# Depthwise convolution as three products over half columns, four channels in four row groups of TensorE

## The chip, the cores and the metric

The kernel runs on one core of a Trainium2 chip. The metric is device time in microseconds (us) of one execution. The median of 13 runs of the kernel before is 4737.9 us (4729.0 to 4768.0). A core has five engines: TensorE (PE, with its weight loads as PEld), VectorE (DVE), ScalarE (ACT), GpSimd (POOL) and SyncE (SP), which in this program only issues DMA transfers. ScalarE and GpSimd issue some transfers too.

## The reference

Two layers in a row, all in float32. The first layer takes x of shape (32 images, 128 channels, 56, 56):

```python
x = conv(input, dw_kernel)          # 7x7, one filter per channel, padding 3
x = layernorm over the 128 channels of each pixel
logits = x @ Wg; top 2 of 8 experts per token, softmax weights, at most CAP tokens an expert
out = input + x + layer_scale * (sum over the token's experts of gate * MLP(x))
```

The second layer is a coordinate attention (two pooled directions, two sigmoid gates), a full 3x3 convolution, a batch norm and a SiLU on the same shape. The change is in the first line alone: y[n, c, h, w] = bias[c] + sum over i, j of k[c, i, j] * x[n, c, h + i - 3, w + j - 3].

## The kernel before

The program runs in stages, and in one instruction order per engine that follows the order of the code where the tile framework's scheduler has no reason to differ. The stages are: the depthwise convolution (lines 99 to 156, writes y_d in HBM), the layer norm with the routing scores (lines 163 to 312, reads y_d back), the experts (gathers, two matrix products and accumulating scatters, lines 613 to 646), and the second layer (from line 802). Only the first is touched.

**The depthwise convolution before.** It takes two channels at a time, 64 pairs. The 56 rows of an image lie on 56 partitions: one channel on partitions 0 to 55, the other on 64 to 119 (`rows`). The free axis of the tile `xt` holds 32 images x 56 columns. A column tap of the filter is a product of `xt`, shifted along the columns, with a banded 56 x 56 matrix (`band`, a diagonal per row tap), so seven taps sum up the 7x7 filter in PSUM. Images are split in two halves, which go to the lower and the upper 64 partitions of the output, so that four matmuls (two channels, two halves) use the four 64 x 64 quarters of the array. An accumulator `acc` holds 2 x 8 images x 56 columns of one channel in one PSUM bank; there are 8 banks, and a pair of channels uses 4 of them, two in each of two turns (`b`).

Around the products:

- SP loads `hk` (the taps, line 123) and `xt` (line 124), one transfer each per channel. `xt` has three buffers, so a load waits until TensorE is done with the pair three before.
- GpSimd reverses `hk` into `band` (line 125).
- ScalarE evicts the accumulator of the first channel with its bias (line 148), VectorE that of the second (line 150), into `yt` (three buffers).
- ScalarE issues the writes of `yt` to y_d: four per pair, of 196 KB each, after the second turn's evictions (line 153). Every run of 56 columns is a packet of 224 B, in the loads of x as in the writes of y_d.

The next stage loads y_d with SP (line 263) and can do so only when the last write has landed.

Transfers that SP and ScalarE issue signal through eight semaphores that they take in turn; a transfer that takes a semaphore again first waits until that semaphore's previous transfer has landed.

Of the kernel before, what the change touches and what calls it, by code (L numbers as in the profile page):

```python
# [8 lines left out]
F32 = mybir.dt.float32  # L9
# [3 lines left out]
AF = mybir.ActivationFunctionType  # L13
ALU = mybir.AluOpType
# [4 lines left out]
N, C, H, W = 32, 128, 56, 56  # L19
# [5 lines left out]
P = 128  # L25
# [14 lines left out]
WIN = 2 * H - 1  # L40


def bc(ap, shape):
    return ap.to_broadcast(shape)
# [3 lines left out]
def moe_conv_then_coordatt_kernel(ctx: ExitStack, tc: tile.TileContext, a: dict, out: bass.AP):  # L48
    nc = tc.nc
# [6 lines left out]
    y_d = dram.tile([N, C, HW], F32, name="y_d")  # L56
# [41 lines left out]

    with ExitStack() as st:
        cp1 = st.enter_context(tc.tile_pool(name="dwc", bufs=1))  # L100
        xp = st.enter_context(tc.tile_pool(name="dwx", bufs=3))
        wp = st.enter_context(tc.tile_pool(name="dww", bufs=3))
        yp = st.enter_context(tc.tile_pool(name="dwy", bufs=3))
        pp = st.enter_context(tc.tile_pool(name="dwp", bufs=8, space=PSUM))

        G = P // 2
        dwb = cp1.tile([P, C], F32, name="dwb")
        nc.sync.dma_start(dwb, a["dw_bias"].rearrange("c h -> (c h)").unsqueeze(0).partition_broadcast(P)
                          .rearrange("p x c -> p (x c)"))
        taps = a["dw_kernel"]  # L110
        NB = 4
        NI = N // NB
        bands = [cp1.tile([P, 7, G], F32, name=f"band_{k}") for k in range(3)]
        for t in bands:
            nc.gpsimd.memset(t, 0.0)
        for cp in range(C // 2):
            hk = wp.tile([P, 7, H], F32, tag="hk", name=f"hk{cp}")
            xt = xp.tile([P, N, W], F32, tag="xt", name=f"xt{cp}")
            band = bands[cp % 3]
            for c in range(2):  # L120
                rows = slice(c * G, c * G + H)
                src = bass.AP(taps.tensor, taps.offset + (2 * cp + c) * 7 * WIN, [[1, H], [WIN, 7], [1, H]])
                nc.sync.dma_start(hk[rows], src)
                nc.sync.dma_start(xt[rows], a["x"][:, 2 * cp + c].rearrange("n h w -> h n w"))
                nc.gpsimd.tensor_copy(band[rows, :, 0:H], hk[rows, :, ::-1])  # L125
            yt = yp.tile([P, 2, N // 2, W], F32, tag="yt", name=f"yt{cp}")
            for b in range(NB // 2):

                acc = [pp.tile([P, NI, W], F32, tag="acc", name=f"acc{cp}_{b}_{c}") for c in range(2)]
                for n, dw in enumerate((3, 0, 1, 2, 4, 5, 6)):  # L130
                    s = dw - 3
                    lo, hi = max(0, -s), W - max(0, s)
                    for half in range(2):
                        im = slice(half * N // 2 + b * NI, half * N // 2 + (b + 1) * NI)
                        for c in range(2):
                            rows = slice(c * G, c * G + H)
                            nc.tensor.matmul(  # L137
                                acc[c][half * G : (half + 1) * G, :, lo:hi],
                                lhsT=band[rows, dw, :],
                                rhs=xt[rows, im, lo + s : hi + s],  # L140
                                start=(n == 0),
                                stop=(n == 6),
                            )
                for c in range(2):
                    ch = c * (C // 2) + cp
                    dst = yt[:, c, b * NI : (b + 1) * NI, :]
                    if c == 0:
                        nc.scalar.activation(dst, acc[c], AF.Identity, bias=dwb[:, ch : ch + 1])
                    else:
                        nc.vector.tensor_scalar(dst, acc[c], dwb[:, ch : ch + 1], None, ALU.add)  # L150
            for half in range(2):
                for c in range(2):
                    nc.scalar.dma_start(
                        y_d[half * N // 2 : (half + 1) * N // 2, 2 * cp + c, :].rearrange("n (h w) -> h n w", h=H),
                        yt[half * G : half * G + H, c],
                    )

    pr_stack = ExitStack()
    prp = pr_stack.enter_context(tc.tile_pool(name="prp", bufs=1))
# [3 lines left out]
    with ExitStack() as st:  # L163
        yp = st.enter_context(tc.tile_pool(name="lny", bufs=2))
        cp1 = st.enter_context(tc.tile_pool(name="lnc", bufs=4))
        qp = st.enter_context(tc.tile_pool(name="lnq", bufs=1))
        xp = st.enter_context(tc.tile_pool(name="lnx", bufs=2))
        sp = st.enter_context(tc.tile_pool(name="lns", bufs=3))
        pp = st.enter_context(tc.tile_pool(name="lnp", bufs=8, space=PSUM))
# [10 lines left out]
        yts = {}  # L180
# [136 lines left out]
    with ExitStack() as st:  # L317
# [242 lines left out]
        cp1 = st.enter_context(tc.tile_pool(name="fc", bufs=1))  # L560
        wp = st.enter_context(tc.tile_pool(name="fw", bufs=2))
        xp = st.enter_context(tc.tile_pool(name="fx", bufs=1))
# [63 lines left out]
        def back(e, i, yt, xg, idx):  # L626

            pb = pbp.tile([P, BLK, C], F32, tag="pb", name=f"pb{e}_{i}")
            for k, (t, n) in enumerate(blocks[i]):
                nc.tensor.transpose(pb[0:n, k, :], yt[:, k * P : k * P + n], ident)  # L630
            nb, t0 = len(blocks[i]), blocks[i][0][0]
            c = max(c for c in range(NC_) if CHUNKS[c] <= i)
            turn_, k_ = (e * NC_ + c) % 2, i - CHUNKS[c]
            yo = yo_all[turn_][k_]
            whole = [x for x in blocks[i] if x[1] == P]
            parts = [(0, len(whole), P)] if whole else []
            parts += [(k, k + 1, n) for k, (t, n) in enumerate(blocks[i]) if n < P]
            for k0, k1, n in parts:
                shape = [n, k1 - k0, C]
                nc.vector.tensor_tensor(yo[0:n, k0:k1, :], pb[0:n, k0:k1, :], bc(xg[0:n, k0:k1, C + e : C + e + 1], shape),  # L640
                                        ALU.mult)
            return yo
# [14 lines left out]
        def load_weights(e):  # L657
            w1 = wp.tile([C, FF], F32, tag="w1", name=f"w1_{e}")
            nc.sync.dma_start(w1, a["W1"][e])
            w2 = wp.tile([P, NF, C], F32, tag="w2", name=f"w2_{e}")  # L660
            nc.sync.dma_start(w2, a["W2"][e].rearrange("(f p) c -> p f c", p=P))
            return w1, w2

        def weights(e, w1, w2):

            nc.gpsimd.tensor_tensor(w2, w2, bc(ls_bc.unsqueeze(1), [P, NF, C]), ALU.mult)
            pb = php.tile([P, BLK * P], F32, tag="ph", name=f"pb_{e}")[:, 0:NF]
            for f in range(NF):
                nc.tensor.matmul(pb[:, f : f + 1], lhsT=w1[:, f * P : (f + 1) * P], rhs=beta_c, start=True, stop=True)
            bias = wp.tile([P, NF], F32, tag="bias", name=f"bias_{e}")  # L670
            nc.vector.tensor_tensor(bias, pb, b1[:, e, :], ALU.add)
            return w1, w2, bias
# [57 lines left out]
        def some_routing(n):  # L730
            nonlocal issued
            n = min(n, len(order) - issued)
            issued += n
            return order[issued - n : issued]
# [39 lines left out]
        w = weights(0, *load_weights(0))  # L774
        for e in range(E):
# [8 lines left out]
            steps = [some_routing(n) for n in PIECES[e > 0]]  # L784
            compute(e, 0, w, steps[0])
            if e + 1 < E:
                w = weights(e + 1, *load_weights(e + 1)), w
            else:
                w = None, w
# [3 lines left out]
            w = w[0]  # L793
# [8 lines left out]
    with ExitStack() as st:  # L802
        cp1 = st.enter_context(tc.tile_pool(name="cc", bufs=1))
        xp = st.enter_context(tc.tile_pool(name="cx", bufs=2))
# [4 lines left out]
        mp = st.enter_context(tc.tile_pool(name="cm", bufs=3))  # L809
# [72 lines left out]
        for k in range(2):  # L882
            t = cp1.tile([C, H + 2, W + 2], F32, name=f"pad{k}")
# [193 lines left out]
```

## Time and profile before

| | |
|---|---|
| median of 13 runs | 4737.9 us |
| profiled execution | 4743.9 us |
| its span | 4742.0 us |
| depthwise convolution: first to last matmul | 9.9 to 676.4 us |
| load of y_d for the next stage issued | 684.0 us |
| PE busy over the span | 3692.5 us (78%) |
| DVE, ACT, POOL busy | 2174.3, 1313.5, 2688.4 us |
| granted TensorE clock, mean over the span and in the convolution | 0.87 and 1.00 |
| DMA in the convolution from 100 to 600 us | 176 GB/s, nearly all packets under 512 B |

How to read it. A fence that begins with a number is a row of a stretch or of the order of time, in microseconds from the span's start. In the list of groups a row gives line, engine, operation, output and inputs by the program's names, partitions x elements, the count, then busy time, the mean of one in ns, and the idle time of the engine in front of these instructions with what ended it. A float32 matmul shows as two records, so 7168 records are 3584 matmuls. Matmuls overlap and their ends are modelled, so "busy" is not "at its peak". An ACTq or SPq row is the time that an engine takes to issue a transfer, not the time that the transfer takes. The DMA share is the mean over 16 DMA engines of the time that packets took, which can pass 1 where packets overlap.

### The profile page before, as it was taken

Reading aid. Unit: us, or ns where it says so; the run is one execution under the profiler, and the core shown is the slowest. Engines: PE = TensorE matmul, PEld = TensorE weight load, DVE = VectorE, ACT = ScalarE, POOL = GpSimd, SP = SyncE. Lnnn points to the kernel's source line nnn. Section 1 sums busy time; section 2 is a strip of 40 time slices with the busy share of each in tenths; the row PEclk is TensorE's granted clock in tenths of the full one; section 3 lists DMA queues with packets and bytes.
Section 4 is the critical chain, followed back from the end, with each engine's and each line's share of the span. In section 5 each row is a group of like instructions: output and inputs, shape, how many; then the busy total and the mean of one; then the engine's idle time right before and its main releaser. Section 6 shows DMA issues by size and latency. Waiting matters only on the chain. (4 is left out here: it accounts for less than half of the span.)

```text
span 4742.0 us, 50118 instructions
## 1 busy us (share of the span) xinstructions
PE 3692.5 (78%) x17669; PEld 2062.6 (43%) x17669; DVE 2174.3 (46%) x4727; ACT 1313.5 (28%) x2555; POOL 2688.4 (57%) x1862
## 2 busy tenths in 40 slices
PE   9999989774167748656765886677664899999999
PEld 4555558774133324333432343233332455555555
DVE  1111108988736526636441110011113878787776
ACT  1111117553012212212222332232221233333333
POOL 1011003344067868767767766787785765666655
PEclk9999999877578878777877898888887999999999
DMA  9999978987222223222323332233335343444432
GB/s 156 176 177 176 177 165 293 336 314 262 83 44 38 38 51 35 39 44 39 41 41 42 39 47 42 48 41 42 47 42 126 124 156 127 150 150 151 148 123 76
DMA packets 866353, 526.90 MB, mean 111 GB/s; under 512 B 543880, under 2 KB 835488, under 8 KB 855648
## 3 DMA queue, kind: packets, MB, share of 16 engines
q1 hardware_dynamic: 504848, 327.79, 24.1%
q0 software_dynamic: 118720, 91.19, 14.1%
q10 hardware_dynamic: 242320, 102.85, 9.6%
q8 instruction: 155, 2.54, 0.2%
q14 instruction: 310, 2.54, 0.2%
HBM read 268.72 MB, written 252.97 MB: 110 GB/s over the span
## 5 line engine op out<-in xcount | busy, mean ns | idle before, releaser
L646 POOL DMA_INDIRECT acc_d<-yo,idx x676 | 1080.8, 1599 | 311.8 <-issue 205.8
L613 PE MATMUL ph<-fxt,w 128*128 128x512 f32 (+1 forms) x1400 | 714.1, 650 | 259.6 <-ACT ht L614 228.3
L614 ACT ACTIVATE ht<-ph,bias 128x512 f32<-128x512 f32 (+1 forms) x700 | 476.9, 683 | 858.9 <-PE ph L613 439.2
L982 PE MATMUL pc<-v,wk 128*128 128x392 f32 x1920 | 696.3, 505 | 3.2 <-POOL v L967 3.2
L137 PE MATMUL acc<-xt,band 56*64 56x424 f32 (+3 forms) x7168 | 666.4, 527 | 2.7 <-DMA xt<-in_x 2.7
L621 PE MATMUL py<-ht,w 128*128 128x512 f32 (+1 forms) x1400 | 649.3, 608 | 0.0
L594 POOL DMA_INDIRECT xg_r<-x_d,idx x556 | 536.9, 966 | 181.4 <-issue 119.9
L613 PEld LDWEIGHTS ph<-fxt,w 128*128 128x128 f32 x1400 | 274.5, 210 | 547.4 <-issue 287.4
L137 PEld LDWEIGHTS acc<-xt,band 56*64 56x64 f32 x7168 | 339.1, 132 | 329.4 <-issue 215.0
L982 PEld LDWEIGHTS pc<-v,wk 128*128 128x128 f32 x1920 | 344.4, 189 | 307.1 <-issue 96.1
L962 POOL TENSOR_TENSOR d<-pad 128x3248 f32<-128x3248 f32 x32 | 228.3, 7136 | 408.5 <-DVE pad L954 408.5
L275 PE MATMUL lnps<-proj,lnyt 128*128 128x136 f32 x1568 | 361.0, 398 | 103.8 <-ACT sq L280 74.5
L640 DVE TENSOR_TENSOR yo<-pb,xg_r 128x512 f32<-128x512 f32 (+2 forms) x147 | 98.3, 671 | 666.6 <-PE pb L630 279.8
L275 PEld LDWEIGHTS lnps<-proj,lnyt 128*128 128x128 f32 x1568 | 349.4, 316 | 116.0 <-ACT sq L280 85.6
L125 POOL COPY band<-hk 56x392 f32<-56x392 f32 x128 | 65.2, 510 | 573.2 <-issue 520.3
L621 PEld LDWEIGHTS py<-ht,w 128*128 128x128 f32 x1400 | 266.2, 199 | 278.6 <-issue 276.7
L150 DVE TENSOR_SCALAR yt<-acc,dwb 128x448 f32<-128x448 f32 x128 | 87.5, 684 | 582.2 <-PE acc L137 353.5
L605 DVE COPY fxt<-pt 128x512 f32<-128x512 f32 (+1 forms) x175 | 119.5, 683 | 493.9 <-PE pt L603 247.5
L623 ACT ACTIVATE fyt<-py,b 128x512 f32<-128x512 f32 (+1 forms) x175 | 119.6, 683 | 813.6 <-PE py L621 472.9
L992 DVE SCALAR_TENSOR_TENSOR y<-pc,y 128x392 f32<-128x392 f32 x640 | 318.2, 555 | 32.4 <-PE pc L982 32.4
L412 PE MATMUL ps_r<-cnt_r,ones 128*128 128x1 f32 x400 | 83.3, 289 | 248.3 <-DVE junk L411 170.5
L630 PE MATMUL pb<-ident,fyt 128*128 128x128 f32 (+1 forms) x696 | 117.7, 295 | 168.5 <-ACT fyt L623 93.2
(221 smaller groups left out, 4512.1 us busy)
## 6 DMA issues: line engine op xcount, KB each, us to landing
x_d<-xn SPq DMA_DIRECT2D x16, 3332.0 KB
xt<-in_x SPq DMA_DIRECT2D x128, 392.0 KB
y_d<-yt ACTq DMA_DIRECT2D x256, 196.0 KB
lnyt<-y_d SPq DMA_DIRECT2D x16, 3136.0 KB
acc_d<-xn SPq DMA_DIRECT2D x16, 3136.0 KB
x<-in_x SPq DMA_DIRECT2D x16, 3136.0 KB
cxn<-acc_d SPq DMA_DIRECT2D x112, 448.0 KB
out<-y ACTq DMA_DIRECT2D x64, 784.0 KB
```

The source lines that it names most:

```text
L137: nc.tensor.matmul(acc[c][half * G : (half + 1) * G, :, lo:hi], lhsT=band[rows, dw, :], rhs=xt[rows, im, lo + s : hi + s], start=(n == 0), ...
L275: nc.tensor.matmul(ps[:, j, :], lhsT=yf[:, self.j0 + g + j, :], rhs=proj, start=True, stop=True)
L594: d = nc.gpsimd.indirect_dma_start(out=xg[0:n, k, :], out_offset=None, in_=x_d[:, :], in_offset=bass.IndirectOffsetOnAxis(ap=idx[0][0:n, t ...
L605: nc.vector.tensor_copy(xt[:, 0:N_], pt[:, 0:N_])
L613: nc.tensor.matmul(ph[:, 0:N_], lhsT=w[0][:, f * P : (f + 1) * P], rhs=xt[:, 0:N_], start=True, stop=True)
L614: nc.scalar.activation(ht[:, f, 0:N_], ph[:, 0:N_], AF.Gelu, bias=w[2][:, f : f + 1])
L621: nc.tensor.matmul(py[:, 0:N_], lhsT=w2[:, f, :], rhs=ht[:, f, 0:N_], start=(f == 0), stop=(f == NF - 1))
L623: nc.scalar.activation(yt[:, 0:N_], py[:, 0:N_], AF.Identity, bias=b2[:, e : e + 1])
L646: d = nc.gpsimd.indirect_dma_start(out=acc_d[:, :], out_offset=bass.IndirectOffsetOnAxis(ap=idxs[e][1][0:n, t : t + 1], axis=0), in_=yo[0: ...
L962: nc.gpsimd.tensor_tensor(d, high, low, ALU.subtract)
L982: nc.tensor.matmul(m[k], lhsT=wk[k][:, dw, :], rhs=v[:, k, rows, dw : dw + W], start=(dw == 0), stop=(dw == 2))
L992: nc.vector.scalar_tensor_tensor(r[x], m[k], f, r[y_], ALU.mult, ALU.add)
```

## The change

The image rows now lie two to a partition: partition g of a channel holds rows 2g and 2g + 1, 28 partitions a channel, and four channels lie on partitions 0 to 27, 32 to 59, 64 to 91 and 96 to 123. A load of x has packets of two rows, 448 B, still 392 KB a channel.

The columns are split into even and odd ones, E and O, 28 each. A row filter of seven taps over all columns is made of three products over half columns: one with the sums E + O and the middle taps, which both output halves need, one with the odd columns and differences of taps, for the even outputs, and one with the even columns, for the odd outputs. The products have 3, 4 and 4 column offsets, and each offset two row parities: 22 products of 16 images x 28 columns, for two image halves, per channel. (Before: 7 taps of 8 images x 56 columns, in two turns, for two halves.)

There are 32 groups of four channels. In a group, each step of a product issues eight matmuls: four channels on four groups of 32 rows of the array, two image halves on two groups of 64 columns. Each channel has an accumulator in a bank of its own, so a product takes four of the 8 banks.

- ScalarE evicts the first product of each channel with the bias into `m0` (4 evictions a group); VectorE evicts the other two, adds `m0` and writes every second column of `yt` (8 a group).
- GpSimd makes three pieces of `band` with a copy and two subtractions and adds up `xs` = E + O (1792 elements a partition) for each group, one group ahead. Before the first group it clears three tiles `xt`, three `hk` and two `band`.
- ScalarE issues the eight writes of a group (196 KB each, as before) after VectorE's evictions of the third product. In the built program ScalarE's order is: four evictions of a group, its eight writes, four evictions of the next group.
- `yt` and `m0` have eight buffers, `xt` and `hk` three, `band` and `xs` two.

Rows of the new code, with the lines of the old one that they replace left out:

```diff
+        PRODUCTS = ((0, (0, -1, 1), -1), (3, (0, -2, -1, 1), -2), (7, (0, -1, 1, 2), -1))
+                nc.sync.dma_start(hk[rows, 1:8, :], bass.AP(taps.tensor, taps.offset + c * 7 * WIN, [[2, GH], [WIN, 7], [1, K1]]))
+                nc.sync.dma_start(xt[rows].rearrange("g n a w -> g n (a w)"),
+                                  a["x"][:, c].rearrange("n (g a) w -> g n (a w)", a=2))
...
+            nc.gpsimd.tensor_copy(band[:, 0:3, 0:K1], back(2, 8))
+            nc.gpsimd.tensor_tensor(band[:, 3:7, 0:K1], back(1, 9), back(0, 8), ALU.subtract)
+            nc.gpsimd.tensor_tensor(band[:, 7:11, 0:K1], back(1, 9), back(2, 9), ALU.subtract)
+            nc.gpsimd.tensor_tensor(xs, xt[:, :, :, 0:W:2], xt[:, :, :, 1:W:2], ALU.add)
...
+            sources = (xs, xt[:, :, :, 1:W:2], xt[:, :, :, 0:W:2])
+            for i, (t0, offsets, least) in enumerate(PRODUCTS):
+                acc = [pp.tile([P, N // 2, WH], F32, tag="acc", name=f"acc{q}_{i}_{r}") for r in range(QC)]
+                steps = [(o, par) for o in offsets for par in range(2)]
+                for n, (o, par) in enumerate(steps):
+                    lo, hi = max(0, -o), WH - max(0, o)
+                    for r in range(QC):
+                        rows = slice(32 * r, 32 * r + GH)
+                        for half in range(2):
                             nc.tensor.matmul(
+                                acc[r][half * M : (half + 1) * M, :, lo:hi],
+                                lhsT=band[rows, t0 + o - least, 1 - par : 1 - par + M],
+                                rhs=sources[i][rows, half * N // 2 : (half + 1) * N // 2, par, lo + o : hi + o],
...
+                for r in range(QC):
+                    if i == 0:
+                        nc.scalar.activation(m0, acc[r], AF.Identity, bias=dwb[:, k : k + 1])
...
+                    else:
+                        nc.vector.tensor_tensor(yts[r][:, :, i - 1 : W : 2], acc[r], common[r], ALU.add)
+                    if i == 2:
+                        for half in range(2):
+                            nc.scalar.dma_start(
+                                y_d[half * N // 2 : (half + 1) * N // 2, c, :].rearrange("n (h w) -> h n w", h=H),
+                                yts[r][half * M : half * M + H],
+                            )
```

More of the change, by code (lines that the diff above doesn't have):

```diff
@@ L100, in moe_conv_then_coordatt_kernel @@
         cp1 = st.enter_context(tc.tile_pool(name="dwc", bufs=1))
-        xp = st.enter_context(tc.tile_pool(name="dwx", bufs=3))
-        wp = st.enter_context(tc.tile_pool(name="dww", bufs=3))
-        yp = st.enter_context(tc.tile_pool(name="dwy", bufs=3))
+        mp = st.enter_context(tc.tile_pool(name="dwm", bufs=8))
+        yp = st.enter_context(tc.tile_pool(name="dwy", bufs=8))
         pp = st.enter_context(tc.tile_pool(name="dwp", bufs=8, space=PSUM))
-        G = P // 2
+        GH, WH, QC = H // 2, W // 2, 4
+        K1 = H + 1
+        NQ_ = C // QC
+        M = P // 2
         dwb = cp1.tile([P, C], F32, name="dwb")
@@ L110, in moe_conv_then_coordatt_kernel @@
         taps = a["dw_kernel"]
[L111 to L114, printed above, removed]
-            nc.gpsimd.memset(t, 0.0)
[L116 to L136, printed above, removed]
@@ new lines, in moe_conv_then_coordatt_kernel, with fetched @@
+        xts = [cp1.tile([P, N, 2, W], F32, name=f"xt{k}") for k in range(3)]
+        xss = [cp1.tile([P, N, 2, WH], F32, name=f"xs{k}") for k in range(2)]
+        hks = [cp1.tile([P, 9, K1], F32, name=f"hk{k}") for k in range(3)]
+        bands = [cp1.tile([P, 11, M + 1], F32, name=f"band{k}") for k in range(2)]
+        for t in xts + hks + bands:
+            nc.gpsimd.memset(t, 0.0)
+        PRODUCTS = ((0, (0, -1, 1), -1), (3, (0, -2, -1, 1), -2), (7, (0, -1, 1, 2), -1))
+        def fetched(q):
+            xt, hk = xts[q % 3], hks[q % 3]
+            for r in range(QC):
+                c = QC * q + r
+                rows = slice(32 * r, 32 * r + GH)
+                nc.sync.dma_start(hk[rows, 1:8, :], bass.AP(taps.tensor, taps.offset + c * 7 * WIN, [[2, GH], [WIN, 7], [1, K1]]))
+                nc.sync.dma_start(xt[rows].rearrange("g n a w -> g n (a w)"),
+                                  a["x"][:, c].rearrange("n (g a) w -> g n (a w)", a=2))
@@ new lines, in prepared @@
+        def prepared(q):
+            xt, hk, band, xs = xts[q % 3], hks[q % 3], bands[q % 2], xss[q % 2]
+            back = lambda k0, k1: hk[:, k0:k1:2, ::-1]
+            nc.gpsimd.tensor_copy(band[:, 0:3, 0:K1], back(2, 8))
+            nc.gpsimd.tensor_tensor(band[:, 3:7, 0:K1], back(1, 9), back(0, 8), ALU.subtract)
+            nc.gpsimd.tensor_tensor(band[:, 7:11, 0:K1], back(1, 9), back(2, 9), ALU.subtract)
+            nc.gpsimd.tensor_tensor(xs, xt[:, :, :, 0:W:2], xt[:, :, :, 1:W:2], ALU.add)
@@ new lines, in moe_conv_then_coordatt_kernel @@
+        fetched(0)
+        fetched(1)
+        prepared(0)
+        for q in range(NQ_):
+            if q + 2 < NQ_:
+                fetched(q + 2)
+            if q + 1 < NQ_:
+                prepared(q + 1)
+            xt, band, xs = xts[q % 3], bands[q % 2], xss[q % 2]
+            sources = (xs, xt[:, :, :, 1:W:2], xt[:, :, :, 0:W:2])
+            common, yts = [], []
+            for i, (t0, offsets, least) in enumerate(PRODUCTS):
[4 more added lines that the diff above has]
+                    for r in range(QC):
+                        rows = slice(32 * r, 32 * r + GH)
+                        for half in range(2):
@@ L137, in moe_conv_then_coordatt_kernel @@
                             nc.tensor.matmul(
-                                acc[c][half * G : (half + 1) * G, :, lo:hi],
-                                lhsT=band[rows, dw, :],
-                                rhs=xt[rows, im, lo + s : hi + s],
+                                acc[r][half * M : (half + 1) * M, :, lo:hi],
+                                lhsT=band[rows, t0 + o - least, 1 - par : 1 - par + M],
+                                rhs=sources[i][rows, half * N // 2 : (half + 1) * N // 2, par, lo + o : hi + o],
@@ L141, in moe_conv_then_coordatt_kernel @@
                                 start=(n == 0),
-                                stop=(n == 6),
+                                stop=(n == len(steps) - 1),
                             )
[L144 to L148, printed above, removed]
-                    else:
-                        nc.vector.tensor_scalar(dst, acc[c], dwb[:, ch : ch + 1], None, ALU.add)
@@ L151, in moe_conv_then_coordatt_kernel @@
[L151 to L156, printed above, removed]
+                for r in range(QC):
+                    c = QC * q + r
+                    if i == 0:
+                        k = (c % 2) * (C // 2) + c // 2
+                        m0 = mp.tile([P, N // 2, WH], F32, tag="m0", name=f"m0{q}_{r}")
+                        nc.scalar.activation(m0, acc[r], AF.Identity, bias=dwb[:, k : k + 1])
+                        common.append(m0)
+                        yts.append(yp.tile([P, N // 2, W], F32, tag="yt", name=f"yt{q}_{r}"))
+                    else:
+                        nc.vector.tensor_tensor(yts[r][:, :, i - 1 : W : 2], acc[r], common[r], ALU.add)
[5 more added lines that the diff above has]
+                            )
```

## The prediction

> **What bounds the kernel now.** I read the slices of the span first: TensorE is 9 in every slice up to about 680 us, so the depthwise convolution, which is all the change touches, is a stage with one limit. Its line in the costliest groups says which. (Busy us and mean ns of one, then the idle time in front and what ended it.)
>
> ```profile
> L137 PE MATMUL acc<-xt,band 56*64 56x424 f32 (+3 forms) x7168 | 666.4, 527 | 2.7 <-DMA xt<-in_x 2.7
> L150 DVE TENSOR_SCALAR yt<-acc,dwb 128x448 f32<-128x448 f32 x128 | 87.5, 684 | 582.2 <-PE acc L137 353.5 <-DMA y_d<-yt 224.2 <-DMA xt<-in_x 4.5
> ```
>
> TensorE waits 2.7 us in 669. Busy is not peak, so I checked the rate in stretches of the stage (length, busy us of PE, PEld, DVE, ACT, POOL with counts, granted clock, DMA share, GB/s):
>
> ```profile
> 14.00:24.00 10.00, 10.00 (x38) 3.66 (x36) 0.00 (x0) 0.63 (x1) 1.53 (x3) 1.00 1.17 161
> 100.00:600.00 500.00, 500.00 (x5492) 256.91 (x5488) 66.96 (x99) 62.01 (x99) 49.95 (x98) 1.00 1.06 176
> 656.00:676.00 20.00, 20.00 (x220) 10.01 (x212) 2.73 (x4) 2.52 (x4) 0.00 (x0) 1.00 0.42 82
> ```
>
> 5492 records in 500 us are 91.0 ns each. A tap is 8 records (two image halves, two channels, two records a matmul): 0.728 us. A pair of channels is 14 taps, 10.2 us; four channels are 20.4 us. The last stretch has almost no loads and the same 91 ns, so TensorE paces the stage, not the DMA. But the DMA is near: 176 GB/s beside a full share, against 161 with loads alone.
>
> The third view decides my forecast: ScalarE's own order of time. It evicts half of the accumulators and also issues the writes of y_d (ACTq rows).
>
> ```profile
> 339.62 0.63 ACT L148 ACTIVATE yt<-acc,dwb 128x448 f32<-128x448 f32 x1 [4.47 <-PE acc L137]
> 340.28 5.32 ACTq L153 DMA_DIRECT2D y_d<-yt  x4
> 345.65 0.63 ACT L148 ACTIVATE yt<-acc,dwb 128x448 f32<-128x448 f32 x1 [5.40 <-DMA y_d<-yt]
> 350.49 4.22 ACTq L153 DMA_DIRECT2D y_d<-yt  x4
> ```
>
> Issuing four writes of 196 KB holds ScalarE for 4.2 to 5.3 us, and the eviction behind them at 345.65 starts only when the fourth is out: it was late. TensorE did not feel it, because it has accumulators for two channel pairs. Without loads the four cost less:
>
> ```profile
> 656.65 3.32 ACTq L153 DMA_DIRECT2D y_d<-yt  x4
> ```
>
> The first two of a run of four take 0.31 and 0.49 us, the third 3.2 (340.28, 340.69 and 341.22 in the same order of time): two fit, and each further one waits until an earlier one has moved.
>
> **The change, part by part.** All sums are against the profiled execution, 4743.9 us, which lies 6.0 above the median of 4737.9.
>
> *TensorE.* A group is now four channels: 22 steps (6, 8 and 8 for the three products) of 4 channels x 2 halves, 16 records a step. The mean width is 433 columns, before 434. If eight pieces of 32 rows by 64 columns run side by side as four pieces of 64 by 64 do now, a step lasts what a tap lasts, 0.727 us: products of 4.4, 5.8 and 5.8 us, a group 16.0 us against 20.4. Over 32 groups that is -141 us. No row shows four row groups; the bounds are this and no gain from packing, 91 ns x 16 = 1.46 us a step. I take the first: the two row groups now show no loss at all, and the weight loads (132 ns, half the time idle) have room. [...]
>
> *VectorE and GpSimd.* 256 evictions with an add at about 0.68 us are 5.5 us a group, and GpSimd's sums (1792 elements at 7136 ns / 3248 of L962: 3.9 us, and three band operations near 0.5 us each) 5.4 us a group. Both lie beside 16 us of TensorE, and the bands are made one group ahead: nothing. Without that cover they would cost 5 us a group.
>
> *Loads.* Half as many packets, of 448 B. A 392 KB load now is 2.5 us alone (161 GB/s). Rows of 512 B are loaded at 289 GB/s near 3652 us; a packet is 1.39 ns at 224 B and 1.77 at 512, so about 1.68 at 448: 1.5 us a load. Bounds: 1.25 (a packet costs the same) and 2.5 (a byte costs the same). The rows are those of the DMA packets between 14 and 24 us (loads of 224 B) and between 3650 and 3654 us (512 B):
>
> ```profile
> DMA packets 7275, 1.61 MB, mean 161 GB/s; under 512 B 7275, under 2 KB 7275, under 8 KB 7275
> DMA packets 2138, 1.16 MB, mean 289 GB/s; under 512 B 47, under 2 KB 2131, under 8 KB 2131
> ```
>
> SP issues them in order and waits for TensorE's last use of the tile; by the built program's semaphores the third and fourth of a group also wait until the second and third write have landed, so all four still fall among the eight writes.
>
> *The ACT queue, the term that decides.* ScalarE's order is now: four evictions of product 0, eight writes, four evictions of the next group's product 0. The eight writes come out together when product 2 is done. The banks are 8, two products' worth, so product 2 of the next group needs those four evictions. Count from t = 0, the last matmul of a group. VectorE evicts the first accumulator by 0.7; the first write is issued at 0.75. Two writes fit; the eighth is out when the sixth has moved. A write alone is 1.23 us (196 KB at 163 GB/s near 660 us). Beside them go the next loads, four, which wait for the same t = 0. Now, loads and writes of a pair would be 6.0 + 4.9 = 10.9 us alone and take about 9.2 of the 10.2 (the share sinks under 0.6 for a microsecond a pair): a factor 0.84. So (6 x 1.23 + 4 x 1.5) x 0.84 = 11.2 us, begun 1.55 us after t = 0 (a write's data start 0.8 us after its issue): the eighth is out at 12.8. Then four evictions at 0.65, to 15.4 with the gaps; then product 2, 5.8 us: the next group ends at 21.2. TensorE itself could have begun product 2 at 10.2, so the wait is about 5 us a group, more than the 4.4 saved. Bounds: writes without any load in the way, 0.9 + 6 x 1.2 = 8.1 us, a group of 17.4; loads at 2.5 us, a group of 24.6. By the rows beside loads (mean of six runs of four: 4.5 us, so 1.8 a further write) it is 0.75 + 0.9 + 10.8 + 2.7 + 5.8 = 21.0. I take 21.2.
>
> [...]
>
> *Start and end.* The stage ends at 676.4, 23 us more than 64 x 10.2. The new one first clears three tiles of 3584 on GpSimd (three of 448 took 1.29 us, so 10.3), then small ones to 18, then loads three more channels and the taps (to 26) and adds (4): first matmul near 30, less 3 us since the first group has no writes ahead of it. Net +3. At the end eight writes, not four, have to land before the next stage's loads: 4 x 1.23, less the eviction order, +4.4.
>
> **Sum:** 32 x (21.2 - 20.4) + 3 + 4.4 = +33 us: 4777 for an execution like the profiled one, 4771 for the median.
>
> **Rivals.**
> 1. *The writes stay out of the way* (faster). If the eight writes leave at their lone price, a group is 17.4 us: 32 x (-3.0) + 7 = -89, median 4649; if the queue holds all eight at once, TensorE paces at 16.0 and it is 4604. For it: 3.32 us without loads. Against it: every row beside loads is above 4.2. It decides the sign below 19.7 us a group.
> 2. *Loads crowd the writes more* (slower still). By the worst row of four (5.3 us, 2.2 a further write) a group is 23.4, with loads at the price of bytes 24.6: +103 to +142, median 4841 to 4880. In the same band: the granted clock. When TensorE stopped at 676 it fell to 0.50, and after the restart it averaged 0.68 over 694 to 700. Should the new wait trip that in each group, 1.9 us x 32 = 61 us come on top of the forecast: 4832. I do not count it, the wait being 3 to 5 us with single evictions in it.
> 3. *The row groups do not pack*: the change doesn't do what it says. 22 x 1.46 = 32 us a group, +378: 5116. Against it: LDWEIGHTS and MATMUL of the four pieces start within some ten nanoseconds of each other in the trace.
>
> **How the numbers follow.** Forecast (20.0 to 22.4 a group) 0.45; rival 1 0.28; rival 2 with the clock 0.20; rival 3 or part of it 0.07. The range 4645 to 4850 takes in 17.4 to 23.6 a group; outside are a stage paced by TensorE alone, the far end of rival 2 and rival 3, together 0.2. A change under 0.3% (14 us) can't be told from none here; that is 19.7 to 20.6 a group: 0.13. Faster 0.30, slower 0.57.
>
> **What would show it.** In the changed kernel: ACTq runs of eight at 11 to 13 us; an idle gap of TensorE before the product-2 matmuls, released by ScalarE's eviction, 3 to 5 us per group; groups of 21 us; 16 records per 0.73 us inside a product. If the gap is missing and the runs of eight are under 8 us, the ACT step is wrong. If steps are over 0.8 us, packing is. If the stage's DMA share is full and TensorE waits for loads instead, the loads are. A first matmul later than 40 us breaks the start term.

## The result, and the profile after

The median of 14 runs is 4869.2 us; the ratio to the kernel before is 1.027 (95% interval 1.026 to 1.029). It is slower, as forecast, but by four times as much as forecast (+131 us, not +33), and outside the range. The profiled execution took 4865.1 us (span 4863.4), 121 more than that of before. The layer norm's first matmul, which I call the stage end below, moved from 694.3 to 824.3 us, by 130; the stages behind it took 4039 us against 4048. So the convolution holds all of it.

The page of the changed kernel, costliest groups, names the wait:

```profile
L157 PE MATMUL acc<-xt,band 28*64 28x448 f32 (+2 forms) x8192 | 535.2, 616 | 123.0 <-ACT m L169 123.0
L173 DVE TENSOR_TENSOR yt<-acc,m 128x448 f32<-128x448 f32 x256 | 142.0, 618 | 655.9 <-ACT m L169 402.6 <-PE acc L157 253.3
```

Before, TensorE waited 2.7 us in this stage. Now the second and third product wait 123 us, all of it for ScalarE's evictions. The order of time of one group shows where (start, length, idle time in front and what ended it):

```profile
342.06 11.69 SPq L127 DMA_DIRECT2D xt<-in_x  x4
342.07 2.22 DVE L173 TENSOR_TENSOR yt<-acc,m 128x448 f32<-128x448 f32 x4 [6.38 <-PE acc L157]
342.73 14.47 ACTq L176 DMA_DIRECT2D y_d<-yt  x8
...
357.31 2.21 ACT L169 ACTIVATE m<-acc,dwb 128x448 f32<-128x448 f32 x4 [22.29 <-DMA xt<-in_x]
...
358.08 9.83 PE L157 MATMUL acc<-xt,band 28*64 28x448 f32 x122 [4.67 <-ACT m L169]
```

The group's last matmul is at 342.0. Four loads and eight writes start together; the eighth write is out at 357.2, the eviction behind it follows, and TensorE begins the third product right after the first of the four evictions. (The row of the eviction names a load of x as what ended its wait; the writes stand in front of it in ScalarE's order, and experiments 5 and 6, which take them out of its way and keep the loads, show which of the two it was.) That is the forecast's mechanism. What it lacked is in the stretches of the same group (length, PE, PEld, DVE, ACT, POOL, granted clock, DMA share, GB/s):

```profile
341.80:346.20 4.40, 4.40 (x106) 3.77 (x98) 2.22 (x4) 0.00 (x0) 0.68 (x1) 1.00 0.66 120
346.20:353.40 7.20, 7.20 (x142) 5.76 (x126) 0.00 (x0) 0.00 (x0) 0.33 (x1) 1.00 1.08 173
353.40:358.05 4.65, 0.01 (x1) 0.00 (x0) 0.08 (x1) 0.74 (x2) 0.58 (x1) 1.00 0.95 187
358.05:360.00 1.95, 1.92 (x16) 1.34 (x24) 1.95 (x4) 1.47 (x3) 0.00 (x0) 0.51 1.10 203
360.00:362.00 2.00, 2.00 (x32) 1.77 (x24) 0.19 (x1) 0.00 (x0) 0.98 (x1) 0.50 0.97 190
362.00:364.00 2.00, 2.00 (x32) 1.81 (x24) 0.00 (x0) 0.00 (x0) 2.00 (x1) 0.50 0.06 8
```

TensorE is idle in one piece, 4.65 us, until the first of the four evictions is done. Behind it the granted clock is 0.5 for 6.8 us: by the start times the steps of 16 records there take 1.4 to 2.0 us, and 0.7 to 0.8 when it is back at 1.0. From the start times of the matmuls, groups 2 to 29 (72.2 to 767.5 us) compare with the forecast like this:

| us, in a group | forecast | measured |
|---|---|---|
| first product | 4.4 | 4.4 |
| second product | 5.8 | 6.5 |
| run of eight writes | 12.05 | 14.2 (13.0 to 16.4) |
| third product begins | 15.4 | 15.9 |
| third product | 5.8 | 8.9 |
| group | 21.2 | 24.8 |

### The profile page after: what moved, and what is told of

The parts are those of the page before. It is cut to its first block, busy times and chain, and to the rows that moved or that the text cites. A ratio compares the mean times of both kernels' runs of the same rounds, so it can differ in the third digit from the quotient of the medians.

```text
span 4863.4 us, 58770 instructions
## 1 busy us (share of the span) xinstructions
PE 3664.0 (75%) x21765; PEld 2253.5 (46%) x21765; DVE 2226.9 (46%) x4855; ACT 1303.5 (27%) x2555; POOL 2782.9 (57%) x1867
## 5 line engine op out<-in xcount | busy, mean ns | idle before, releaser
L157 PE MATMUL acc<-xt,band 28*64 28x448 f32 (+2 forms) x8192 | 535.2, 616 | 123.0 <-ACT m L169 123.0
L157 PEld LDWEIGHTS acc<-xt,band 28*64 28x64 f32 x8192 | 413.0, 147 | 222.5 <-issue 152.8
L173 DVE TENSOR_TENSOR yt<-acc,m 128x448 f32<-128x448 f32 x256 | 142.0, 618 | 655.9 <-ACT m L169 402.6
L169 ACT ACTIVATE m<-acc,dwb 128x448 f32<-128x448 f32 x128 | 70.7, 635 | 714.8 <-DMA xt<-in_x 431.7
```

Of the source, the lines that this page charges most:

```text
L157: nc.tensor.matmul(acc[r][half * M : (half + 1) * M, :, lo:hi], lhsT=band[rows, t0 + o - least, 1 - par : 1 - par + M], rhs=sources[i][row ...
L173: nc.vector.tensor_tensor(yts[r][:, :, i - 1 : W : 2], acc[r], common[r], ALU.add)
```

## The experiments

Theory A: the order of ScalarE makes the gap, and the gap the half clock; without them TensorE paces at 17.4 us. Rival B: once the gap is gone, the transfers pace. Rival C: the slow third product is contention, not the clock. The kernel before took 4754 to 4782 us beside these runs, and the stages behind the convolution vary by some 35 us from one execution to the next, so I compare stage ends and group times within the stage, and whole times only as ratios.

**1. Writes behind the evictions, in the code only** (e1_writes_later)

```diff
                     if i == 2:
-                        for half in range(2):
-                            nc.scalar.dma_start(
...
+                        late.append((c, yts[r]))
+                if i == 0 or (i == 2 and q == NQ_ - 1):
+                    for c, yt in late:
+                        for half in range(2):
+                            nc.scalar.dma_start(
...
+                    late = []
```

> Edit: the eight writes of a group are issued after ScalarE's four evictions of the next group's first product, not before them; nothing is left out. In the changed kernel a group of four channels takes 24.8 us: first product 4.4, second 6.5, idle gap 4.9, third 8.9 (half clock for about 6.8 us after the gap). Theory A (the eviction queued behind eight writes makes the gap, and the gap makes the half clock): gap and half clock go, a group is 4.4 + 6.5 + 6.5 = 17.4 us, the profiled 4865 falls by 31 x 7.3 = 226 to about 4640. Rival B (the transfers of a group, 3.14 MB, keep the DMA busy for about 20 of the 24.8 us and pace the stage next): a group of 19 to 20 us, TensorE waits for accumulators or for x instead, 4865 - 31 x 5.3 = 4700, between 4685 and 4720.

The ratio was 1.021 (1.017 to 1.025), stage end 790.7, a group 23.8 us. Neither number came, because the edit did not do what it says. ScalarE's order of time:

```profile
332.56 13.47 ACTq L180 DMA_DIRECT2D y_d<-yt  x7
346.13 0.63 ACT L170 ACTIVATE m<-acc,dwb 128x448 f32<-128x448 f32 x1 [22.57 <-DMA y_d<-yt]
346.42 0.68 ACTq L180 DMA_DIRECT2D y_d<-yt  x1
346.67 1.68 ACT L170 ACTIVATE m<-acc,dwb 128x448 f32<-128x448 f32 x3
```

Seven writes are still in front of the evictions, since the tile framework's scheduler does not keep to the order of the code here. The run tells nothing of A against B.

**2. Work in place of the gap** (e2_zero_steps)

```diff
-        bands = [cp1.tile([P, 11, M + 1], F32, name=f"band{k}") for k in range(2)]
+        bands = [cp1.tile([P, 12, M + 1], F32, name=f"band{k}") for k in range(2)]
...
+                if i == 1:
+                    for n in range(6):
+                        for r in range(QC):
...
+                                nc.tensor.matmul(
+                                    acc[r][half * M : (half + 1) * M, :, :],
+                                    lhsT=band[rows, 11, 0:M],
+                                    rhs=xs[rows, half * N // 2 : (half + 1) * N // 2, n % 2, :],
+                                    start=False,
+                                    stop=(n == 5),
```

> Edit: six more steps with an all-zero band at the end of the second product (96 records more a group, 4.4 us), so that TensorE works through most of the gap; the output is the same. Theory A (the half clock follows from the idle gap): the gap shrinks from 4.9 to 0.5 us, the third product runs at full clock, 6.5 us in place of 8.9, and the group falls to 4.4 + 6.5 + 4.4 + 0.5 + 6.5 = 22.3 us although TensorE does more: 4865 - 31 x 2.5 = 4788. Rival C (the slow steps of the third product come from what goes on beside them, evictions and transfers, not from the idleness): it stays at 8.9, the group at 24.7, the time at 4865.

Ratio 1.021 (1.018 to 1.024), stage end 797.5 against 824.3, a group 23.4 us (groups 2 to 29): 96 records more in each group, and the stage is 27 us shorter. Stretches of one group: first product, second with the zero steps, third.

```profile
311.60:316.00 4.40, 4.40 (x107) 4.32 (x99) 2.22 (x4) 0.00 (x0) 0.67 (x1) 1.00 0.64 122
316.00:328.20 12.20, 11.76 (x237) 6.68 (x221) 0.02 (x1) 0.69 (x2) 0.92 (x2) 1.00 0.99 173
328.30:335.40 7.10, 7.10 (x134) 4.78 (x138) 2.10 (x4) 1.43 (x3) 3.17 (x1) 1.00 0.61 109
```

The clock stays at 1.00 and the third product takes 7.1 us in place of 8.9, beside the same evictions and no fewer transfers (109 GB/s here; 93 beside the third product at half clock in the changed kernel, 358.05 to 366.6 us). In three groups a gap of 1.0 to 2.4 us was left, the clock fell, and the third product took 8.5 to 8.7 us. Rival C falls; the half clock costs 1.8 us a group. I had expected 6.5 for that product: it starts on the first of four evictions and then waits for the other banks one by one, some 0.8 us.

**3. No loads** (e3_no_loads; the `dma_start` of `hk` and `xt` only for q < 3)

> Edit: x and the taps are loaded for the first three groups only, later groups use what lies in the tiles (leaves out the other channels of x). It prices the writes without loads beside them. Theory A (the writes are long because loads share the DMA): a run of eight takes 0.9 + 6 x 1.2 = 8.1 us, not 14; evictions done 11.6 us after the group's end, gap under 1 us, no half clock, a group of 17.4 to 18.3: 4865 - 29 x 6.9 = about 4665. Rival (eight writes take this long by themselves): runs of eight stay above 12 us and the group above 23.

Stage end 622.0, a group 17.4 us (groups 4 to 16), as theory A has it:

```profile
283.69 9.05 ACTq L178 DMA_DIRECT2D y_d<-yt  x8
292.85 2.21 ACT L171 ACTIVATE m<-acc,dwb 128x448 f32<-128x448 f32 x4 [15.75 <-DMA y_d<-yt]
```

A run of eight is 8.5 us in the mean of these groups (7.5 to 9.1), near the forecast's bound without loads, 8.1. The loads beside it make the other 5.7 of 14.2 us. Over groups 2 to 29 a group is 17.6 us.

**4. One contiguous source** (e4_one_source: the first edit, and `sources = (xs, xs, xs)`)

> Edit: as the first of these (writes after the evictions), and all three products read the contiguous sums xs, none the even or odd columns of xt (leaves out the difference products' inputs). It tells why a step of the second and third product takes 0.80 us where one of the first takes 0.73. Theory S (reading every second column costs it): all steps take 0.73, second and third product 5.8 us each in place of 6.5. Rival (the transfers or the weights cost it): they stay at 6.4 to 6.5. The group is 16.0 us if TensorE paces, and as in the first of these if the DMA does.

Second and third product, a group in which neither waited:

```profile
346.05:351.85 5.80, 5.80 (x142) 4.69 (x132) 0.00 (x0) 2.14 (x4) 0.78 (x2) 1.00 1.08 197
351.85:357.68 5.83, 5.83 (x141) 4.03 (x130) 2.22 (x4) 0.07 (x1) 0.59 (x1) 1.00 1.12 188
```

5.8 us, theory S. With every second column they take 6.25 to 6.3 at best (experiments 3 and 9, full clock), so the stride costs 0.5 us a product. (Experiment 12, which copies these columns into runs, comes back to 5.8.) The groups vary from 16.0 to 24.7 us and the stage ends at 686.6: the first sign of B.

**5. The order enforced** (e5_ordered: the first edit, and an edge without a semaphore from the last eviction to each write `d`)

```diff
-                        nc.scalar.activation(m0, acc[r], AF.Identity, bias=dwb[:, k : k + 1])
+                        last = nc.scalar.activation(m0, acc[r], AF.Identity, bias=dwb[:, k : k + 1]).ins
...
+                            if i == 0:
+                                tc.add_manual_dep(d.ins, last.name, mybir.DependencyInfo(
+                                    mybir.DependencyClass.NoSync, mybir.DependencyReason.DATA), reason="order")
```

> Edit: the eight writes are issued after the next group's four evictions, this time with an order edge for each write, since without it the built order kept seven of the eight in front. Nothing is left out. Theory A (only ScalarE's order makes the gap and the half clock): a group is 4.4 + 6.5 + 6.5 = 17.4 us, stage end (first matmul of the layer norm) 824 - 31 x 7.1 = 604 us. Rival B (the DMA paces once the gap is gone: with the products sped up by reading one source only, it moved 174 GB/s at a share of 0.97, and the groups took 19.9 us on the mean): groups of 19 to 20.5 us, stage end 665 to 710 us, DMA share over 0.95, idle time of TensorE released by loads or by accumulators late for that reason.

Ratio **0.990** (0.987 to 0.993), stage end 665.9, a group 19.3 us. The order of time and the stretch from 200 to 600 us:

```profile
344.49 2.21 ACT L170 ACTIVATE m<-acc,dwb 128x448 f32<-128x448 f32 x4 [17.58 <-DMA y_d<-yt]
...
347.36 15.96 ACTq L180 DMA_DIRECT2D y_d<-yt  x8
```

```profile
200.00:600.00 400.00, 384.94 (x7210) 265.14 (x7200) 91.18 (x161) 44.20 (x80) 97.05 (x83) 0.98 1.06 176
```

The whole loss was the order of one queue: the same work, four evictions in front of eight writes, takes 3.6% less time than the changed kernel (0.990 to 1.027) and 1% less than the kernel before. But not at 17.4 us: it stops at a share of 1.06 and 176 GB/s, the very numbers of the kernel before (1.06 and 176 from 100 to 600 us). What TensorE then waits for most are the sums of x, and GpSimd, which makes them, waits for the loads:

```profile
L158 PE MATMUL acc<-xs,band 28*64 28x432 f32 (+1 forms) x3072 | 172.6, 534 | 26.9 <-POOL xs L136 24.4 <-issue 2.3
L136 POOL TENSOR_TENSOR xs<-xt 128x1792 f32<-128x1792 f32 x32 | 101.6, 3174 | 378.3 <-DMA xt<-in_x 360.8 <-DMA y_d<-yt 13.9 <-DMA hk<-in_dw_kernel 3.6
```

That is rival B; experiment 9 tests it.

**6. Evictions on VectorE** (e6_vector_evicts: `nc.vector.tensor_scalar(m0, acc[r], dwb[:, k : k + 1], None, ALU.add)`)

> Edit: the first product's four evictions go to VectorE (12 x 0.63 = 7.6 us of a group), ScalarE only issues the writes, right at the group's end as in the changed kernel. Nothing is left out. It takes the wait away without moving the writes. Theory A: no gap from evictions, no half clock, 17.4 us a group, stage end 604 us. Rival B (the DMA paces): 19 to 20.5 us a group, stage end 665 to 710 us, as in the ordered version; what TensorE then waits for is x or the sums made from x.

Ratio 0.993 (0.991 to 0.996), stage end 674.6, a group 19.5 us. With no evictions on ScalarE at all, TensorE waits for the sums of x instead:

```profile
L157 PE MATMUL acc<-xs,band 28*64 28x432 f32 (+1 forms) x3072 | 180.4, 601 | 61.5 <-POOL xs L136 59.9 <-DVE yt L173 1.4
```

**7. Loads on two queues** (e7_two_queues: the fifth, with `(nc.gpsimd if r % 2 else nc.sync).dma_start(xt...)`)

> Edit: the ordered version, and the loads of the second and fourth channel of a group go out from GpSimd's queue, so that loads of different partitions can be under way together. Nothing is left out. If loads are slow because one channel at a time (28 partitions) is read, two at a time are faster and the group falls by up to 2.5 us against the ordered version. Rival (the bytes or packets of all transfers together set the rate): no gain, or a loss, within 1 us a group of the ordered version.

Stage end 687.3, a group 19.8 us, 174 GB/s: no gain. (The first matmul comes 4.5 us later than in the fifth.)

**8. Half of x in as many packets** (e8_half_packets: `xt[rows, :, 0, :]` alone is loaded)

> Edit to the changed kernel: only the even image rows of x are loaded, as many packets as before but of 224 B in place of 448 (leaves out the odd rows of x). It tells what a load costs by. The forecast priced a 448-B load at 1.5 us because 512-B packets had cost little more than 224-B ones elsewhere. Theory F (a packet costs, the forecast's reading): the loads before the first matmul take as long as in the changed kernel (a channel with its taps 2.8 us), runs of eight writes stay near 14 us, the group near 24.8. Theory G (bytes cost, 154 to 159 GB/s for loads alone there): a channel's load falls from 2.5 to 1.25 us, runs of eight to about 11, the eviction is done at 13 after the group's end and not 16, the gap falls to about 2 us and the group to about 21.5: stage end near 720 us.

Before the first matmul a channel with its taps goes out every 1.6 us; it was 2.9. Runs of eight last 11.7 us in the mean:

```profile
272.82 11.85 ACTq L176 DMA_DIRECT2D y_d<-yt  x8
284.77 2.21 ACT L169 ACTIVATE m<-acc,dwb 128x448 f32<-128x448 f32 x4 [18.54 <-DMA y_d<-yt]
```

Theory G: a load of this shape costs by its bytes, and the forecast's 1.5 us should have been its own upper bound, 2.5. The group took 22.3 us (21.5 expected; stage end 750.9, not 720), because gaps of 2.5 us from matmul start to matmul start, 1.9 of them idle, were left in the mean, and the half clock still came 25 times in 31.

**9. The same half loads in the right order** (e10_ordered_half)

> Edit: the ordered version with the same half loads (leaves out the odd rows of x). Theory B (the DMA paces the ordered version at 176 GB/s): 2.4 MB a group are 13.7 us, so TensorE paces, 17.0 to 17.4 us a group, stage end 600 us, full clock throughout, DMA share under 0.95. If it stays near 19.4 us a group, it is not the amount of data but the order of ScalarE, VectorE and the queues that paces the ordered version.

Every group takes 16.97 us, stage end 593.5:

```profile
200.00:500.00 300.00, 300.00 (x6232) 144.20 (x6224) 78.24 (x142) 39.73 (x72) 85.00 (x71) 1.00 0.98 156
```

So it is the amount of data that holds the ordered version at 19.3 us. (The share is 0.98 even here; I had expected less. The share alone does not tell a bound from a near-bound.)

**10. An earlier start** (e9_start: the first x tile cleared in halves by GpSimd and VectorE, taps and bands by VectorE, the other x tiles afterwards)

> Edit: the ordered version, and at the start only the first x tile is cleared before the first loads, half by GpSimd and half by VectorE, VectorE clears the taps and bands, the other x tiles follow. Nothing is left out. The first load goes out near 9 us as before, but the second and later ones follow at once instead of at 17.6: first matmul near 25 us, not 31, stage end about 6 us earlier than in the ordered version (666), near 660, since the DMA paces from its first byte. Against the kernel before: 0.985 to 0.99 of its time. If the stage end does not move, the start is hidden by the prefetch.

First matmul at 26.8 us in place of 31.4, stage end 658.3, 7.6 earlier. Ratio 0.991 (0.988 to 0.994), just short of what I expected and not to be told from the fifth: the gain is shown by the stage end only.

**11. Packets of 512 B** (e11_wide_packets: the tenth, and `bass.AP(x, c * HW, [[2 * W, GH], [C * HW, N], [1, 128]])` into a tile 128 wide)

> Edit: the version with the early start, and each packet of x is 512 B long, the two rows and 64 B after them that nothing uses (the last channel excepted). Nothing is left out. Loads alone moved 154 GB/s with packets of 224 B and 155 with 448 B, but 289 GB/s with 512 B later in the program. Theory T (from 512 B on a packet costs less): a channel's load falls from 2.6 to 1.6 us although it moves 14% more, the DMA's work of a group from 19.4 to about 16 us, and TensorE paces at 17.0: stage end near 595 us in place of 658, time against before 0.975 to 0.98. Rival (bytes cost the same at any size, the later rate was due to 128 partitions): a load takes 2.9 us, the group about 20.3, stage end near 685 us.

Ratio **0.986** (0.983 to 0.989), stage end 632.6, a group 18.2 us: the best of all, and yet theory T fell. Alone, the loads moved 157 GB/s, as before, and a channel with its taps took 3.2 us; at that rate the load itself is 2.9, the rival's price. But the rival's group of 20.3 us did not come either. The gain is beside the writes:

```profile
200.00:600.00 400.00, 392.63 (x7756) 240.11 (x7745) 99.44 (x176) 49.57 (x90) 97.67 (x84) 0.99 1.03 197
```

197 GB/s in place of 176, more than the 64 B of padding in each packet make up for. Why packets of 512 B get along better with the writes, no run here shows.

**12. Odd and even columns copied apart** (e12_copied_halves: two `nc.gpsimd.tensor_copy` a group into tiles of their own)

> Edit: as the version with 512-B packets, and GpSimd copies the odd and the even columns into tiles of their own, so that all products read runs of columns (two more GpSimd operations of 1792 elements a group, 2 to 3 us each beside 16 us). Nothing is left out. If the steps fall from 0.80 to 0.73 and the DMA lets it, a group is 16.0 to 16.5 us, stage end near 570 us; if the DMA or GpSimd paces, it stays with the other version.

Steps fell to 0.73 and groups without transfers took 16.0 us, but the others 20 us: ratio 0.995 (0.993 to 0.998), stage end 680.5, worse than the eleventh. DMA moved 184 GB/s, not 197, and GpSimd was busy 42% of the time in place of 24%. Whether its copies slow the transfers or VectorE was not tried.

**13. Loads by themselves** (e13_load_prices)

```diff
+        tests = [cp1.tile([P, N, 128], F32, name=f"test{k}") for k in range(3)]
+        for rows, width in ((28, 56), (56, 56), (112, 56), (28, 112), (56, 112), (112, 112), (112, 128)):
+            for k in range(3):
+                nc.sync.dma_start(tests[k][0:rows, :, 0:width],
+                                  bass.AP(a["x"].tensor, a["x"].offset + 4 * k * HW,
+                                          [[min(width, 112), rows], [C * HW, N], [1, width]]))
```

> Edit to the changed kernel: before the first group, 21 loads of x into tiles that nothing reads, three each of 28, 56 and 112 partitions with packets of 224 B, the same with 448 B, and 112 partitions with 512 B; the convolution starts after them. Nothing is left out. It measures the disputed price of a load by itself. So far loads of 28 partitions moved 154, 155 and 157 GB/s with packets of 224, 448 and 512 B, and loads of 56 partitions with 224 B 161. Theory P (with packets of 448 B the number of partitions sets it): 448 B on 56 and 112 partitions move far more, 250 GB/s and up, 224 B on 112 partitions stay near 160. Rival Q (the size of a packet does not matter under some 512 B, nor do the partitions): everything with 224 and 448 B stays at 150 to 165 GB/s, and only 512 B on 112 partitions reaches 289.

DMA packets in seven stretches, in the order of the list above (10 to 13, 17 to 23, 28 to 34, 38 to 44, 50 to 56, 66 to 76 and 86 to 98 us):

```profile
DMA packets 1911, 0.42 MB, mean 141 GB/s; under 512 B 1911, under 2 KB 1911, under 8 KB 1911
DMA packets 3690, 0.82 MB, mean 137 GB/s; under 512 B 3690, under 2 KB 3690, under 8 KB 3690
DMA packets 4402, 0.98 MB, mean 163 GB/s; under 512 B 4402, under 2 KB 4402, under 8 KB 4402
DMA packets 2180, 0.96 MB, mean 161 GB/s; under 512 B 2180, under 2 KB 2180, under 8 KB 2180
DMA packets 2472, 1.10 MB, mean 183 GB/s; under 512 B 2472, under 2 KB 2472, under 8 KB 2472
DMA packets 5450, 2.43 MB, mean 243 GB/s; under 512 B 5450, under 2 KB 5450, under 8 KB 5450
DMA packets 5199, 2.65 MB, mean 220 GB/s; under 512 B 32, under 2 KB 5199, under 8 KB 5199
```

The first row is rough: these loads take only 5 us, and the rate falls within them from 245 to 90 GB/s. Neither theory holds whole. Packets of 448 B move 161, 183 and 243 GB/s on 28, 56 and 112 partitions, a rise as in theory P, but short of its 250; 224 B move 141, 137 and 163. The 183 and 243 are outside rival Q's 150 to 165 as well, and 512 B on 112 partitions, for which it had 289, move 220, no more than 448. The size of a load grows with its partitions here (196 to 1792 KB), so this run does not part the two: at the same 392 KB, 28 partitions with packets of 448 B moved 161 GB/s and 56 with 224 B 137. What it does show is the disputed price: a load of 28 partitions with 448 B goes at 161 GB/s, as in the changed kernel itself (155), and not at the 268 GB/s that 1.5 us would be. The change doubled the packet and halved the partitions, 56 to 28, and in the two kernels' own loads the rate stayed about the same, 161 and 155.

The whole time of this kernel, 4969.8 us, holds the added loads and is not compared.

## Why the prediction was wrong

The sign and the mechanism were right: runs of eight writes, the evictions behind them, a gap in front of the third product. The size was wrong by 3.6 us a group, which are, by the runs: third product at half clock 1.8 (experiment 2), banks handed over one by one 0.8 (2), every second column in the third product 0.5 (4), and a start of it 0.5 later. Thirty-two times 3.6 would be 115 us; the forecast was off by 98, since the first two and the last two groups, with little or no gap, are some 20 us shorter together, of which the sum had 3.

- **The clock: this is the step that failed.** "I do not count it, the wait being 3 to 5 us with single evictions in it." The gap was 4.9 us from matmul start to matmul start as forecast (123 us of idle time over the groups, 4.2 each), and the clock fell behind it 29 times; the price I gave in the rival, 1.9 us, was right (1.8). The single evictions did not break up the wait: they come at its end, and up to the first of them TensorE is idle in one piece. I put gap and clock in separate cases, though filling the gap keeps the clock up (2): 4771 + 61 = 4832 should have been the forecast. That is still 37 short of 4869, by the other three terms.
- **Loads.** "So about 1.68 at 448: 1.5 us a load" is refuted (8, 13): about 2.6. I interpolated in packet size between loads of 56 partitions and loads of another shape, and took no account of the number of partitions or the size of the load. The run of eight was 2.2 us longer than forecast. (With 2.6 us a load the forecast's own formula gives a run of 15.7 us, so its factor for the overlap, 0.84, was too high beside eight writes, where 14.2 was measured.) The longer run shifted the group by only 0.5, because TensorE went on after one eviction where I had it wait for all four.
- **Packing.** Right: the first product takes 4.4 us, 0.73 a step of 16 records against 0.728 a tap of 8 before, so four row groups show no loss against the two of before. "A step lasts what a tap lasts" missed the stride of the second and third product, 0.80.
- **VectorE and GpSimd at nothing:** right, neither released the wait. **Start:** first matmul forecast near 30, measured 31.5. **End:** last matmul to stage end 20.6 us against 18.0, +2.6 for +4.4.
- **Rival 1** (writes at their lone price, 17.4 us a group) is what a group takes without loads (3), but in part by luck: it let the evictions pace the group, and there TensorE's own products did, 4.4, 6.5 and 6.7 us almost without a gap. **Rival 2** held the number, 24.8 against its far end of 24.6, by luck too: its dear loads moved the group by only 0.5, the clock, which it named apart, by 1.8, and the other 1.3 it did not have.
- **What I did not see** is that the saving was bounded from the start. TensorE would pace at 17.0 (9), but the bytes stay nearly the same, and 176 GB/s at a full share, which I quoted, leave 19.3 us a group whatever the order (5, 6, 7 and 10: 19.2 to 19.8) as long as the packets are these (11). Of the 141 us that the sum gave the change, some 35 could be had by it alone.

## What to carry to other kernels

When one engine evicts and also issues transfers, the order of its queue is the first thing to place, and to check in the built program, not in the code: here it decided between 2.7% slower and 1% faster than before. A gap that a forecast itself predicts has to be priced with the clock that follows it, which cost 1.8 us a group here. When the bound engine gets faster, take the next resource at its rate over the whole stage (bytes by the measured GB/s) as a floor, and price a transfer by a row of the same shape, with as many partitions and as many bytes, not only with as long packets: those of 448 B moved 161 to 243 GB/s in experiment 13.

## What the runs showed of the hardware that I had not expected

- TensorE's gaps and the clock, over the profiles of all these kernels: of 106 gaps of 2.3 us or more of idle time between two matmuls of the stage, 104 were followed by a granted clock of 0.5, among them all 78 of 3.2 us or more; of 76 gaps of 1.2 to 2.3 us, 58 were. The two exceptions are 2.6 us (experiment 7) and 3.1 us (experiment 12), with a clock of 1.00 behind them, so the length of the gap alone does not decide; what else does, no run here shows. The gap of experiment 12 and what follows it:

```profile
333.20:336.40 3.20, 0.10 (x3) 0.01 (x1) 0.68 (x2) 0.00 (x0) 2.39 (x2) 1.00 1.09 161
336.40:339.00 2.60, 2.60 (x56) 1.28 (x64) 2.07 (x4) 0.00 (x0) 0.00 (x0) 1.00 1.17 180
```

- A float32 matmul whose moving columns lie 8 bytes apart took 8% longer than with contiguous ones (6.28 and 5.80 us for the same product; experiments 9 and 4).
- Loads of x padded to 512 B raised the mixed traffic from 176 to 197 GB/s, while alone they gained nothing (157 against 155 GB/s).
